# Unscaled rows scattered with three numbers behind each, in a layernorm, scan, attention and expert block

## The chip, the cores and the metric

The kernel runs on one core of one Trainium2 chip. The metric is the device time of one launch in microseconds. PE is TensorE (PEld its weight loads), DVE VectorE, ACT ScalarE, POOL GpSimd and SP SyncE; each takes its instructions in order, and so do the queues on which SP and POOL issue transfers.

## The reference

The input x is (8, 512, 256) in fp32: 8 batches of 512 rows. The result is x + scan(xn) + ffn(xn), where xn is the layernorm of x. What is computed, cut to its core:

```python
# scan branch: A, Bp, Cp, Dp drive a linear recurrence over the 512 rows
u = xn @ W_in + b_in                    # 256 -> 512 channels
u = causal depthwise conv of width 4 (u) + conv_b
h = tanh(A) @ h + u_t * Bp;  y_t = Cp . h + Dp * u_t
scan = silu(y) @ W_out + b_out
# ffn branch: attention plus experts
q, k, v = split(xn @ W_qkv + b_qkv)     # 16 heads of 16
attn = softmax(q k^T / 4) v
gate = softmax(xn @ W_gate + b_gate)    # 8 experts
top_g, top_i = top_k(gate, 2)
moe = sum over the 2 picked experts of top_g * (xn @ W_experts[e] + b_experts[e])
x + scan + attn + moe
```

## The kernel before

**Tiles.** Rows go by 128 on the partitions: NTT = 32 tiles of 128 rows, NT = 4 in each of B = 8 batches. D is 256, E is 8, NJ is 4 (the 256 features as 4 times 64, so that two 64-row matmuls run in two halves of TensorE's rows at a time), S is 512.

**Scan branch.** The recurrence is a lower triangular Toeplitz matrix for each batch (tile ps_zx), followed by the projection with conv (ps_z, L1346; cw is the conv's weights, ys its result on DVE, L1361), a silu by tanh on ACT (th, L1355 and L1371) and the output projection (ps_o, L1384).

**Attention.** There are 32 groups i of 4 heads (4 groups a batch), each in 8 steps s: 256 steps. In a step TensorE forms the scores for the row maximum (maxima, ps_mx, L1533), DVE reduces them (reduce_max, mx, L1545), TensorE forms the transposed scores less that maximum (weights, ps_p, L1571 and L1579), ACT takes the exponential (exponent, p, L1589), and TensorE multiplies by v (values, av, L1598). At the end of a group ACT copies av (av_sb), TensorE transposes it (ps_at), DVE divides by the sums (norm_scale, rsum L1630 and attn L1631) and POOL adds the result to the batch's sum (norm_add, acc, L1641). The q and k of a group come by 16 transfers on SP (load_stack, qs and ks, L1501) from arrays that SP stored before (split, L1480).

**Routing.** With all gates known, DVE picks the two highest of each row (route_pick), counts rows by expert (route_count on TensorE, route_totals), gives each of the 8192 chosen rows a slot in an array sorted by expert (route_slots, key r7) and finds the places to be filled with zeros (route_pads) and the expert of each pair of tiles (wrow, L1139; key r8).

**Experts.** The sorted array xs_d holds NPAIR = 36 pairs of 128-row tiles, each pair of one expert. For each batch, POOL loads the normalised rows (scatter_load, xr, L1163, 512 KB), ACT multiplies each by its gate (scatter_scale, xs, L1170) and POOL scatters them by indirect transfers of 128 rows (place, L1154; 64 for the slots, 16 for the pads). After all of these, each pair is worked on: POOL loads its rows (moe_load, xg, L1189, in 256 B runs) and its expert's weights (wt, L1194, an indirect transfer); TensorE transposes the rows (moe_transpose by turn and tp2, ps_xg, L138 in halves, L150 in whole) with the rows as its stationary operand; ACT copies the result (xgT, L1208); TensorE multiplies (moe_mult, ps_e, L133, a helper's line that other products share); ACT copies (moe_result, y, L1216); SP stores (moe_store, y_d, L1219). In the end POOL gathers the two results of each row and adds them to the batch's sum (combine_gather, L1233). The biases of the experts are added elsewhere, by a small product with the gates (combT).

**Order.** All engines' programs are written in one order by a planner (plan, run_all). Each piece of work is an op: engine, estimated duration, due time "at" in attention steps, the keys that it needs and makes, and the buffers of a ring that it takes and frees. The planner simulates the engines by these estimates, with several settings, and keeps the shortest plan; where TensorE would stand still for long it puts in matmuls on nothing (idle_work, ps_idle, L366). The rings that matter here are attn (2), p (8), xt (2, for xr), big (2, for the scaled rows), stack0 and stack1 (3, the groups' q and k), xg, w, xgT and y (2 each). Changed estimates shift the order of all engines.

Of the kernel before, what the change touches and what calls it, by code (L numbers as in the profile page):

```python
# [12 lines left out]
F32 = mybir.dt.float32  # L13
# [10 lines left out]
def ssm_attention_moe_block(  # L24
# [53 lines left out]
    nc = tc.nc  # L78
# [23 lines left out]
    ppool = ctx.enter_context(tc.tile_pool(name="ppool", bufs=8))  # L102
# [74 lines left out]
    def reach(at):  # L177
# [5 lines left out]
        "m": 3, "mx_m": 1, "p_m": 2, "av": 1, "p": 8, "parts": 2, "mrow": 2, "th": 2, "avsb": 2, "attn": 2,  # L183
# [318 lines left out]
    pad = const.tile([P, 2 * E], I32, name="pad")  # L502
# [516 lines left out]
    def route_pick(i):  # L1019
# [6 lines left out]
        m = tiny("r0", NTT)  # L1026
# [6 lines left out]
        else:  # L1033
            nc.vector.tensor_tensor(rt["z", 2], rt["z", 0], oh, ALU.add)
            nc.vector.tensor_tensor(gates, rt["z", 2], gl, ALU.mult)

# [65 lines left out]
    def route_pads():  # L1102
# [3 lines left out]
        at, lim = tiny("at", 2 * E), tiny("lim", 2 * E)  # L1106
        nc.vector.tensor_tensor(at[:, 0:E], begin_row, count, ALU.add)
        nc.vector.tensor_tensor(
            at[:, E : 2 * E], step[:, 0:E], end[:, E - 1 : E].to_broadcast([P, E]), ALU.add
        )  # L1110
        nc.vector.tensor_scalar(at[:, E : 2 * E], at[:, E : 2 * E], float(P), None, ALU.mult)
        nc.vector.tensor_scalar(at, at, lane, None, ALU.add)
        nc.vector.tensor_scalar(lim[:, 0:E], end, float(P), None, ALU.mult)
        nc.vector.memset(lim[:, E : 2 * E], float(ROWS))
        yield
        ok, spare = tiny("ok", 2 * E), tiny("spare", 2 * E)
        nc.vector.tensor_tensor(ok, at, lim, ALU.is_lt)
        nc.vector.tensor_scalar(spare, step[:, 0 : 2 * E], float(P), float(ROWS), ALU.mult, ALU.add)
        nc.vector.tensor_scalar(spare, spare, lane, None, ALU.add)
# [14 lines left out]
        nc.vector.tensor_reduce(ex, cmp, AX.X, ALU.add)  # L1134

# [8 lines left out]
    NW = 2 * NTT + 2 * E  # L1144
    xs_d = nc.dram_tensor("xs_d", [ROWS + 2 * E * P, D], F32, kind="Internal").ap()
# [15 lines left out]
    def scatter_load(b):  # L1161
        xr[b] = wk2.tile([P, NT, D], F32, tag="x", name=f"xr_{b}")
        nc.gpsimd.dma_start(out=xr[b], in_=rows_of(xn_d[b]))  # L1163

    def scatter_scale(b, i):

        xg_of[b, i] = wk2.tile([P, NT, D], F32, tag="big", name=f"xs_{b}_{i}")
        for t in range(NT):
            n = b * NT + t
            nc.scalar.mul(  # L1170
                xg_of[b, i][:, t, :].rearrange("p (j d) -> p j d", j=NJ),
                xr[b][:, t, :].rearrange("p (d j) -> p j d", j=NJ),
                top[:, i, n : n + 1],
            )
# [695 lines left out]
```

## Time and profile before

| what | value |
|---|---|
| times of three runs | 831.86, 830.24, 823.12 us (median 830.24) |
| profiled execution | 832.42 us, its span 830.7 us, mean granted clock 0.975 |
| busy: PE, DVE, ACT, POOL | 774.7, 534.7, 481.2, 322.6 us |
| the chain that ended last | PE 75%, DVE 9%, ACT 6%, "another core or an unknown queue" 3% |
| scaled copies on ACT (L1170) | 64 of 751 ns, first at 203.2 us, last at 347.5 |
| scatters on POOL (L1154) | 64 of 1036 ns for slots, first at 204.3 us, last at 353.2; 16 for pads |
| loads of sorted rows on POOL (L1189) | 36 of 1318 ns, first at 360.6 us, last at 656.2 |
| gathers of results on POOL (L1233) | 64 of some 1.6 us, nearly all after 680 us |

A span runs from the first to the last instruction of the profiled execution; the time has a little more around it. Busy times are of one engine; "idle before" is the time in which an engine stood before an instruction, put down to what released it. A chain of waits is followed back from the last instruction, and "another core or an unknown queue" is a piece whose releaser the profile can't name. The granted clock is a share of TensorE's full speed.

### The profile page before, as it was taken

How to read it: one execution, taken by the hardware profiler on the slowest of the kernel's cores; microseconds unless marked ns; L12 is line 12 of the kernel's file. 1: busy time of each engine (PE TensorE's matmuls, PEld its weight loads, DVE VectorE, ACT ScalarE, POOL GpSimd, SP SyncE). 2: the span in 40 equal slices, each digit the busy share in tenths (PEclk: the TensorE clock that was granted, in tenths of full speed). 3: DMA queues.
4: the chain of work that ended last, by engine and by line, in shares of the span. 5: the costliest groups of instructions: out<-in, count | busy, mean ns of one | idle time of the engine just before them, and what ended most of it. 6: DMA issues, size and time to landing. Idle time of an engine off the chain costs nothing.

```text
span 830.7 us, 15673 instructions
## 1 busy us (share of the span) xinstructions
PE 774.7 (93%) x6076; PEld 484.3 (58%) x6076; DVE 534.7 (64%) x797; ACT 481.2 (58%) x663; POOL 322.6 (39%) x323
## 2 busy tenths in 40 slices
PE   9998899999897589989999999999999999999997
PEld 8665555555553345446655667665666665555644
DVE  2767776699662474883548654564875557859683
ACT  2536776657775265853656655665575556537363
POOL 4001111011657484543333332332231218388884
PEclk9999999999799598999999999999999999999999
DMA  6757677344656255466967868795855957879754
GB/s 141 200 171 226 165 232 185 98 113 157 188 158 204 82 159 184 130 173 215 239 171 215 221 188 232 191 275 140 251 143 154 258 183 146 234 142 191 150 93 111
DMA packets 115806, 147.67 MB, mean 178 GB/s; under 512 B 33644, under 2 KB 78740, under 8 KB 115733
## 3 DMA queue, kind: packets, MB, share of 16 engines
q1 hardware_dynamic: 93460, 95.28, 40.5%
q0 software_dynamic: 22272, 51.39, 24.8%
q8 instruction: 48, 0.79, 0.4%
q14 instruction: 26, 0.20, 0.1%
HBM read 95.24 MB, written 51.38 MB: 176 GB/s over the span
## 4 chain that ended last, share of the span: by engine, by line
PE 75%; DVE 9%; ACT 6%; another core or an unknown queue 3%; issue 2%; SPq 2%; DMA 1%; POOL 0%; DVEq 0%; ACTq 0%; POOLq 0%
PE av L1598 11%; PE ps_mx L1533 8%; PE ps_p L1571 8%; PE ps_e L133 8%; PE ps_o L1384 7%; PE ps_z L1346 6%; PE ps_p L1579 6%; DVE mx L1545 5%; PE ps_qk L133 5%; PE ps_zx L133 4%; ACT p L1589 3%; PE ps_v L133 3%; PE ps_idle L366 2%; SPq L1501 2%
## 5 line engine op out<-in xcount | busy, mean ns | idle before, releaser
L1545 DVE TENSOR_REDUCE mx<-ps_mx 128x2 f32<-128x1024 f32 x256 | 312.6, 1221 | 180.5 <-PE ps_mx L1533 128.0
L1589 ACT ACTIVATE p<-ps_p 128x1024 f32<-128x1024 f32 x256 | 258.1, 1024 | 95.9 <-PE ps_p L1579 84.0
L1533 PE MATMUL ps_mx<-ks,qs 64*128 64x512 f32 x512 | 124.7, 468 | 22.8 <-DVE mx L1545 18.3
L1571 PE MATMUL ps_p<-qs,ks 64*128 64x512 f32 x512 | 124.2, 472 | 20.9 <-remote 8.7
L1598 PE MATMUL av<-p,v_aug 128*32 128x512 f32 x1024 | 123.3, 599 | 0.0
L1641 POOL TENSOR_TENSOR acc<-acc,attn 128x256 f32<-128x256 f32 x32 | 28.1, 898 | 200.7 <-DVE attn L1631 156.7
L1579 PE MATMUL ps_p<-mrow,pick 64*128 64x512 f32 x512 | 105.2, 397 | 0.0
L1533 PEld LDWEIGHTS ps_mx<-ks,qs 64*128 64x128 f32 x512 | 52.1, 187 | 80.6 <-DVE mx L1545 28.4
L1571 PEld LDWEIGHTS ps_p<-qs,ks 64*128 64x128 f32 x512 | 50.7, 188 | 76.5 <-issue 27.2
L1154 POOL DMA_INDIRECT xs_d<-xs,slot x64 | 66.3, 1036 | 68.0 <-ACT xs L1170 54.2
L1233 POOL DMA_INDIRECT res<-y_d,slot x48 | 76.6, 1595 | 24.2 <-issue 17.6
L1189 POOL DMA_DIRECT2D xg<-xs_d x36 | 47.4, 1318 | 83.3 <-PE ps_xg L138 31.9
L1361 DVE SCALAR_TENSOR_TENSOR ys<-th,cw,ys 128x511 f32<-128x511 f32 (+2 forms) x96 | 72.8, 758 | 1.5
L133 PE MATMUL ps_e<-wt,xgT 64*128 64x256 f32 x576 | 69.6, 380 | 0.0
L1346 PE MATMUL ps_z<-zx,wi 128*128 128x512 f32 x128 | 65.3, 633 | 0.3 <-issue 0.2
L1194 POOL DMA_INDIRECT wt<-in_L_ffn_W_experts_dram,wrow x36 | 35.8, 995 | 68.5 <-PE ps_e L133 29.5
L1384 PE MATMUL ps_o<-wo,ys 128*128 128x256 f32 x256 | 62.1, 387 | 0.0
L133 PEld LDWEIGHTS ps_e<-wt,xgT 64*128 64x128 f32 x576 | 54.3, 186 | 12.6 <-issue 2.3
L1598 PEld LDWEIGHTS av<-p,v_aug 128*32 128x32 f32 x1024 | 26.8, 109 | 54.4 <-issue 53.3
L1579 PEld LDWEIGHTS ps_p<-mrow,pick 64*128 64x128 f32 x512 | 51.4, 189 | 4.6
L1384 PEld LDWEIGHTS ps_o<-wo,ys 128*128 128x128 f32 x256 | 47.4, 194 | 5.4
L133 PE MATMUL ps_qk<-xnTr,wqkv_sb 64*128 64x256 f32 x384 | 47.9, 388 | 2.7 <-ACT xs L1170 1.6
(205 smaller groups left out, 952.1 us busy)
## 6 DMA issues: line engine op xcount, KB each, us to landing
split<-parts SPq DMA_DIRECT2D x32, 512.0 KB
qs<-split SPq DMA_DIRECT2D x248, 64.0 KB
ks<-split SPq DMA_DIRECT2D x248, 64.0 KB
xg<-xs_d POOLq DMA_DIRECT2D x36, 256.0 KB
y_d<-y SPq DMA_DIRECT2D x36, 256.0 KB
xn_d<-xn SPq DMA_DIRECT2D x32, 128.0 KB
acc<-in_L_attn_x_dram SPq DMA_DIRECT2D x8, 512.0 KB
xnr<-xn_d SPq DMA_DIRECT2D x16, 256.0 KB
```

Of the source, the lines that this page charges most:

```text
L133: mm(o, lhsT=lhs, rhs=rhs, start=(j == 0), stop=(j == len(parts) - 1))
L1154: nc.gpsimd.indirect_dma_start(out=xs_views[view], out_offset=bass.IndirectOffsetOnAxis(ap=index, axis=0), in_=src, in_offset=None,)
L1233: nc.gpsimd.indirect_dma_start(out=to[:, t, :], out_offset=None, in_=y_d[:, :], in_offset=bass.IndirectOffsetOnAxis(ap=slot[:, h, n : n + ...
L1346: mm(held["z", b, ct], lhsT=wi[:, c, ct * P : (ct + 1) * P], rhs=zx[b][:, c, :], start=(c == 0), stop=(c == ND - 1),)
L1361: nc.vector.scalar_tensor_tensor(y[:, lag:S], held["th", b, ct][:, 0 : S - lag], cw[:, ct, k : k + 1], bias_tab[:, ct, :] if lag == 0 else ...
L1384: mm(o, lhsT=ys[b][:, ct, t * P : (t + 1) * P], rhs=wo[:, ct, :], start=False, stop=(ct == NCT - 1),)
L1533: mm(ps[:, u, :], lhsT=qs[i % 3][64 * u : 64 * u + 64, pr, t * P : (t + 1) * P], rhs=ks[i % 3][64 * u : 64 * u + 64, pr, :], start=True, s ...
L1545: nc.vector.tensor_reduce(mx[i][:, t, 2 * pr : 2 * pr + 2], held["x", i, s], AX.X, ALU.max, negate=True)
L1571: mm(ps[:, u, :], lhsT=ks[i % 3][64 * u : 64 * u + 64, pr, t * P : (t + 1) * P], rhs=qs[i % 3][64 * u : 64 * u + 64, pr, :], start=True, s ...
L1579: mm(ps[:, u, :], lhsT=pick[64 * u : 64 * u + 64, pr, :], rhs=held["mrow", i, pr][64 * u : 64 * u + 64, :], start=False, stop=True,)
L1589: nc.scalar.activation(p, held["s", i, s], AF.Exp, scale=SCALE)
L1598: mm(av[i][j * HW : (j + 1) * HW, :], lhsT=v_aug[b % 2][:, t, o : o + HW], rhs=pm[i, 2 * t + j // 2][:, j % 2, :], start=(t == 0), stop=(t ...
```

## The change

- Rows are scattered as they are, not scaled. Each row in xs_d is 259 numbers (1036 B) in place of 256: behind the features stand the difference of the two gates, the second gate, and the rank of the first expert. ACT's 64 scaled copies are gone, and the scatters take their rows from xr itself.
- xr is loaded by SP in place of POOL. POOL copies the three numbers behind each row (scatter_tail).
- The pads take 8 transfers in place of 16. route_pads gets a running sum over the experts for it.
- Before the first pair, SP loads all the three-number tails of the sorted rows (tails_load, 9216 runs of 12 B), and DVE makes a gate for each sorted row from them (tails_dve, gate_s): the first gate where the pair's rank is the row's, else the second.
- Sorted rows are loaded by SP in runs of 1 KB (moe_rows); only the weights stay on POOL. The transposes then read every fourth number of a row.
- moe_result is two ACT multiplications by gate_s, 128x256 each, in place of one copy of 128x512.
- The attn ring has 4 buffers in place of 2, the p ring 7 in place of 8. The planner's estimates of the scatters, the loads and the gathers change (0.97 to 1.27, 3.9 to 7.3).

The diff, cut to what matters:

```diff
-    ppool = ctx.enter_context(tc.tile_pool(name="ppool", bufs=8))
+    ppool = ctx.enter_context(tc.tile_pool(name="ppool", bufs=7))
...
-        "m": 3, "mx_m": 1, "p_m": 2, "av": 1, "p": 8, "parts": 2, "mrow": 2, "th": 2, "avsb": 2, "attn": 2,
+        "m": 3, "mx_m": 1, "p_m": 2, "av": 1, "p": 7, "parts": 2, "mrow": 2, "th": 2, "avsb": 2, "attn": 4,
...
@@ -499,7 +499,12 @@
     gates = const.tile([P, NTT, E], F32, name="gates")
     top = const.tile([P, 2, NTT], F32, name="top")
     slot = const.tile([P, 2, NTT], I32, name="slot")
-    pad = const.tile([P, 2 * E], I32, name="pad")
+    pad = const.tile([P, E], I32, name="pad")
+    tails = const.tile([P, NTT, 3], F32, name="tails")
+    ranks = const.tile([P, 2 * NPAIR], F32, name="ranks")
+    gate_s = const.tile([P, 2 * NPAIR], F32, name="gate_s")
     wrow = const.tile([P, NPAIR], I32, name="wrow")
     lane_i = const.tile([P, 1], I32, name="lane_i")
@@ -1023,7 +1028,7 @@
         nc.vector.tensor_tensor(eq, src, wide(top[:, i, :]), ALU.is_equal)
         yield
         nc.vector.tensor_tensor(eq, eq, over(rank), ALU.mult)
-        m = tiny("r0", NTT)
+        m = tails[:, :, 2] if i == 0 else tiny("r0", NTT)
         nc.vector.tensor_reduce(m, eq, AX.X, ALU.max)
         yield
         nc.vector.tensor_tensor(oh, eq, wide(m), ALU.is_equal)
@@ -1033,6 +1038,8 @@
         else:
             nc.vector.tensor_tensor(rt["z", 2], rt["z", 0], oh, ALU.add)
             nc.vector.tensor_tensor(gates, rt["z", 2], gl, ALU.mult)
+            nc.vector.tensor_tensor(tails[:, :, 0], top[:, 0, :], top[:, 1, :], ALU.subtract)
+            nc.vector.tensor_copy(tails[:, :, 1], top[:, 1, :])
     def route_count():
         both = rt["z", 2].rearrange("p t e -> p (t e)")
@@ -1103,20 +1110,27 @@
+        at, lim, none = tiny("at", E), tiny("lim", E), tiny("none", E)
...
+        left, more = tiny("left", E), tiny("more", E)
+        nc.vector.tensor_scalar(left, none, float(P), None, ALU.add)
+        k = 1
+        while k < E:
+            nc.vector.tensor_copy(more[:, 0:k], left[:, 0:k])
+            nc.vector.tensor_tensor(more[:, k:E], left[:, k:E], left[:, 0 : E - k], ALU.add)
+            left, more = more, left
+            k *= 2
...
@@ -1132,6 +1146,7 @@
         yield
         ex = tiny("ex_of", n)
         nc.vector.tensor_reduce(ex, cmp, AX.X, ALU.add)
+        nc.vector.tensor_scalar(ranks, ex, -1.0, float(E), ALU.mult, ALU.add)
         nc.vector.tensor_scalar(ex, ex, float(E - 1), float(P // 2), ALU.min, ALU.mult)
         nc.vector.tensor_scalar(ex, ex, lane64, None, ALU.add)
@@ -1141,8 +1156,10 @@
             )
-    NW = 2 * NTT + 2 * E
-    xs_d = nc.dram_tensor("xs_d", [ROWS + 2 * E * P, D], F32, kind="Internal").ap()
+    NW = 2 * NTT + E
+    XW = D + 3
+    xs_d = nc.dram_tensor("xs_d", [ROWS, XW], F32, kind="Internal").ap()
     xs_views = dram_disjoint_views(xs_d, NW)
     y_d = dram.tile([ROWS, D], F32, name="y_d")
     part_d = dram.tile([B, S, D], F32, name="part_d")
@@ -1159,36 +1176,46 @@
         )
     def scatter_load(b):
-        xr[b] = wk2.tile([P, NT, D], F32, tag="x", name=f"xr_{b}")
-        nc.gpsimd.dma_start(out=xr[b], in_=rows_of(xn_d[b]))
-    def scatter_scale(b, i):
-        xg_of[b, i] = wk2.tile([P, NT, D], F32, tag="big", name=f"xs_{b}_{i}")
-        for t in range(NT):
-            n = b * NT + t
-            nc.scalar.mul(
-                xg_of[b, i][:, t, :].rearrange("p (j d) -> p j d", j=NJ),
-                xr[b][:, t, :].rearrange("p (d j) -> p j d", j=NJ),
-                top[:, i, n : n + 1],
-            )
+        xr[b] = wk2.tile([P, NT, XW], F32, tag="x", name=f"xr_{b}")
+        nc.sync.dma_start(out=xr[b][:, :, 0:D], in_=rows_of(xn_d[b]))
+    def scatter_tail(b):
+        nc.gpsimd.tensor_copy(xr[b][:, :, D:XW], tails[:, b * NT : (b + 1) * NT, :])
     def scatter(b, t, i):
         n = b * NT + t
-        place(2 * n + i, slot[:, i, n : n + 1], xg_of[b, i][:, t, :])
+        place(2 * n + i, slot[:, i, n : n + 1], xr[b][:, t, :])
     def set_zero():
-        rt["zero"] = wk2.tile([P, 2, D], F32, tag="y", name="zero")
+        rt["zero"] = wk2.tile([P, 2, D], F32, tag="y", name="zero").rearrange("p u d -> p (u d)")[:, 0:XW]
         nc.gpsimd.memset(rt["zero"], 0.0)
     def scatter_pads(j):
-        place(2 * NTT + j, pad[:, j : j + 1], rt["zero"][:, 0, :])
+        place(2 * NTT + j, pad[:, j : j + 1], rt["zero"])
+    def tails_load():
+        rt["tails"] = wk2.tile([P, 4 * D], F32, tag="big", name="tails_s")[:, 0 : 3 * 2 * NPAIR]
+        nc.sync.dma_start(
+            out=rt["tails"].rearrange("p (i w) -> p i w", w=3),
+            in_=xs_d.rearrange("(i p) w -> p i w", p=P)[:, :, D:XW],
+        )
+    def tails_dve():
+        v = rt["tails"].rearrange("p (i w) -> p i w", w=3)
+        nc.vector.tensor_tensor(gate_s, v[:, :, 2], ranks, ALU.is_equal)
+        nc.vector.tensor_tensor(gate_s, gate_s, v[:, :, 0], ALU.mult)
+        nc.vector.tensor_tensor(gate_s, gate_s, v[:, :, 1], ALU.add)
+    def moe_rows(k):
+        xg[k] = wk2.tile([P, 2 * D], F32, tag="xg", name=f"xg_{k}")
+        nc.sync.dma_start(
+            out=xg[k].rearrange("p (u d) -> p u d", u=2),
+            in_=xs_d[2 * k * P : 2 * (k + 1) * P, 0:D].rearrange("(u p) d -> p u d", u=2),
+        )
     def moe_load(k):
-        xg[k] = wk2.tile([P, NJ, 2, P // 2], F32, tag="xg", name=f"xg_{k}")
-        nc.gpsimd.dma_start(
-            out=xg[k], in_=xs_d[2 * k * P : 2 * (k + 1) * P, :].rearrange("(u p) (j d) -> p j u d", u=2, j=NJ)
-        )
         wt[k] = wk2.tile([P, NJ, D], F32, tag="w", name=f"wt_{k}")
         nc.gpsimd.indirect_dma_start(
@@ -1200,7 +1227,7 @@
     def moe_transpose(k):
         held["xg", k] = turn(
-            f"ps_xg_{k}", [lambda r, j=j: xg[k][r, j].rearrange("p u d -> p (u d)") for j in range(NJ)]
+            f"ps_xg_{k}", [lambda r, j=j: xg[k][r].rearrange("p (m j) -> p j m", j=NJ)[:, j, :] for j in range(NJ)]
         )
     def moe_evict(k):
@@ -1213,7 +1240,9 @@
     def moe_result(k):
         res["y", k] = wk2.tile([P, 2, D], F32, tag="y", name=f"y_{k}")
-        nc.scalar.copy(res["y", k], held["e", k][:, :, 0:D])
+        for u in range(2):
+            n = 2 * k + u
+            nc.scalar.mul(res["y", k][:, u, :], held["e", k][:, u, 0:D], gate_s[:, n : n + 1])
     def moe_store(k):
         nc.sync.dma_start(
@@ -1266,27 +1295,31 @@
     def scatter_ops(b, at):
         X = ("xt", "xr", b)
-        op("pool", 0.83, at, lambda: scatter_load(b), needs=[("xn_d", b), "r7"], makes=[("xr", b)], takes=[X], kb=512)
+        op("sp", 0.5, at - 2, lambda: scatter_load(b), needs=[("xn_d", b), "r2"], makes=[("xr", b)], takes=[X], kb=512)
+        op("pool", 0.25, at, lambda: scatter_tail(b), needs=[("xr", b), "r4"], makes=[("xt", b)])
         for i in range(2):
-            G = ("big", "xs", b, i)
-            op("act", 1.5, at, lambda i=i: scatter_scale(b, i), needs=[("xr", b)], makes=[("xs", b, i)], takes=[G], frees=[X])
             for t in range(NT):
-                op("pool", 0.97, at, lambda t=t, i=i: scatter(b, t, i), needs=[("xs", b, i)], makes=["placed"], frees=[G], kb=128)
+                op("pool", 1.27, at, lambda t=t, i=i: scatter(b, t, i), needs=[("xt", b), "r7"], makes=["placed"], frees=[X], kb=128)
         if b == B - 1:
             Z = ("y", "zero")
             op("pool", 0.52, at, set_zero, makes=["zero"], takes=[Z])
-            for j in range(2 * E):
-                op("pool", 0.97, at, lambda j=j: scatter_pads(j), needs=["zero", "r8"], makes=["placed"], frees=[Z], kb=128)
+            for j in range(E):
+                op("pool", 1.27, at, lambda j=j: scatter_pads(j), needs=["zero", "r8"], makes=["placed"], frees=[Z], kb=128)
     placed = "all_placed"
     def moe_ops(k, at):
         G, W, T, Y = ("xg", k), ("w", k), ("xgT", k), ("y", k)
-        op("pool", 1.8, at - 3, lambda: moe_load(k), needs=[placed] + reach(at - 8), makes=[("moe", k)], takes=[G, W], kb=768)
-        op("pe", 0.5, at, lambda: moe_transpose(k), needs=[("moe", k)], makes=[("moet", k)], takes=[("mt", "xg", k), T], frees=[G])
+        if k == 0:
+            Z = ("big", "tails")
+            op("sp", 0.4, at - 4, tails_load, needs=[placed], makes=["tails"], takes=[Z], kb=700)
+            op("dve", 0.5, at - 3, tails_dve, needs=["tails", "r8"], makes=["gate_s"], frees=[Z])
+        op("sp", 0.4, at - 3, lambda: moe_rows(k), needs=[placed] + reach(at - 8), makes=[("moex", k)], takes=[G], kb=256)
+        op("pool", 1.27, at - 3, lambda: moe_load(k), needs=["r8"] + reach(at - 8), makes=[("moew", k)], takes=[W], kb=512)
+        op("pe", 0.5, at, lambda: moe_transpose(k), needs=[("moex", k)], makes=[("moet", k)], takes=[("mt", "xg", k), T], frees=[G])
         op("act", 0.59, at, lambda: moe_evict(k), needs=[("moet", k)], makes=[("moeT", k)], frees=[("mt", "xg", k)])
-        op("pe", 1.75, at, lambda: moe_mult(k), needs=[("moeT", k)], makes=[("moep", k)], takes=[("m", "e", k), Y], frees=[W, T])
-        op("act", 0.59, at, lambda: moe_result(k), needs=[("moep", k)], makes=[("moey", k)], frees=[("m", "e", k)])
+        op("pe", 1.75, at, lambda: moe_mult(k), needs=[("moeT", k), ("moew", k)], makes=[("moep", k)], takes=[("m", "e", k), Y], frees=[W, T])
+        op("act", 0.85, at, lambda: moe_result(k), needs=[("moep", k), "gate_s"], makes=[("moey", k)], frees=[("m", "e", k)])
         op("sp", 0.4, at + 0.5, lambda: moe_store(k), needs=[("moey", k)], makes=[("y_d", k)], frees=[Y], kb=256)
     def combine_ops(b, at):
@@ -1298,7 +1331,7 @@
         into = ("acc", b) if late else ("res", b)
         for h in range(2):
             op(
-                "pool", 3.9, at - 3 + h, lambda h=h: combine_gather(b, h),
+                "pool", 7.3, at - 3 + h, lambda h=h: combine_gather(b, h),
                 needs=ys_all + reach(at - 6 + h) + [("moe_in", b, h - 1) if h else into], makes=[("moe_in", b, h)], kb=512,
             )
         if not late:
-        o = held["attn", i] = wk2.tile([P, 4 * NT * HD], F32, tag="attn", name=f"attn_{i}", bufs=2)
+        o = held["attn", i] = wk2.tile([P, 4 * NT * HD], F32, tag="attn", name=f"attn_{i}", bufs=4)
```

## The prediction

> **What bounds the kernel now.** I read the page's totals and its 40 slices first.
>
> ```profile
> span 830.7 us, 15673 instructions
> PE 774.7 (93%) x6076; PEld 484.3 (58%) x6076; DVE 534.7 (64%) x797; ACT 481.2 (58%) x663; POOL 322.6 (39%) x323
> PE   9998899999897589989999999999999999999997
> POOL 4001111011657484543333332332231218388884
> PEclk9999999999799598999999999999999999999999
> ```
>
> TensorE is the bound almost everywhere; only slices 11 to 14 (some 205 to 310 us) fall to 7, 5 and 8, and there POOL rises and the granted clock drops. So I asked for the busy time by window.
>
> ```profile
> core 0: us, PE busy (x) PEld busy (x) DVE busy (x) ACT busy (x) POOL busy (x), PEclk, DMA share, GB/s
> 120.00:200.00 80.00, 77.28 (x622) 44.12 (x618) 61.25 (x132) 50.38 (x73) 7.58 (x16) 1.00 0.51 147
> 200.00:260.00 60.00, 55.17 (x364) 33.92 (x364) 39.32 (x54) 44.09 (x62) 36.07 (x36) 0.91 0.54 171
> 260.00:320.00 60.00, 40.61 (x223) 22.50 (x216) 30.18 (x42) 30.52 (x43) 36.57 (x38) 0.77 0.42 132
> 320.00:365.00 45.00, 41.53 (x265) 21.21 (x263) 33.37 (x42) 32.02 (x45) 24.79 (x25) 0.96 0.49 157
> 500.00:680.00 180.00, 177.17 (x1469) 116.43 (x1466) 108.41 (x131) 105.44 (x141) 45.00 (x42) 1.00 0.75 208
> ```
>
> Columns: stretch, length, busy time of each engine, granted clock. From 500 on TensorE is 98% busy with the experts mixed in. From 200 to 365, while rows are scattered, it isn't. Taking off the fill matmuls of L366 (5.37, 0.60 and 0 us there, 2.54 before 200) and multiplying by the clock, an estimate of work at full clock: 49.80 x 0.91 + 40.01 x 0.77 + 41.53 x 0.96 = 45.3 + 30.8 + 39.9 = 116.0 us in 165, or 70%. The 80 us before have (77.28 - 2.54)/80 = 93%. The loss is some 40 us, and I looked for its causes in the groups (line, what it writes from what, shapes, count | busy us, mean ns | idle before) and in the chain of waits, by time (start, us, what).
>
> ```profile
> L1170 ACT ACTIVATE xs<-xr,top 128x256 f32<-128x256 f32 x64 | 42.9, 751 | 0.0
> L823 ACT ACTIVATE xn<-x,rs 128x256 f32<-128x256 f32 x32 | 16.9, 590 | 7.0 <-POOL rs L815 6.8
> L1154 POOL DMA_INDIRECT xs_d<-xs,slot x64 | 66.3, 1036 | 68.0 <-ACT xs L1170 54.2
> L1189 POOL DMA_DIRECT2D xg<-xs_d x36 | 47.4, 1318 | 83.3 <-PE ps_xg L138 31.9
> L138 PEld LDWEIGHTS ps_xg<-ident,xg 64*128 64x128 f32 x232 | 11.2, 138 | 6.2 <-ACT p L1589 1.6 <-issue 1.5 <-PE ps_mx L1533 0.5
> ```
>
> ```profile
> 261.54 10.15 another core or an unknown queue
> 271.71 0.26 DVE rsum L1630
> ...
> 275.51 7.66 another core or an unknown queue
> 283.20 1.24 DVE mx L1545
> ```
>
> Two causes show. POOL's scatters stand 54.2 us waiting for ACT's scaled copies, and ACT's in-order queue holds those copies (four per group, 2.6 us on the chain at 218 and 236 us) between the exponentials that TensorE needs. And there are the pieces without a releaser, 18.7 us of chain between 195 and 290: VectorE waits for matmuls long started, and goes on (271.71, 283.20) near the end of a run of back-to-back scatters and pads on POOL (250.9 to 281.4 us).
>
> **The change, part by part.**
>
> *Scaling taken off ACT.* 64 copies, 42.9 us of ACT in 150 us, are gone, with the waits of scatter on copy and of copy on the "big" buffers. Scatters then follow POOL's own pace, 0.96 + 0.30 us: 72 x 1.27 = 91 us in place of 204 to 354. For the stretch I take the rate of 320 to 365, where scatters still run but no piece without a releaser shows: 39.9/45 = 88.6%. 116.0/0.886 = 130.9 us against 165: -34.1. The bounds are 0 (nothing of the loss was due to it) and the 93% of before 200: 116.0/0.934 = 124.2, -40.8. The attn ring of 4 belongs here: POOL's adds L1641 stand between scatters, and DVE's next group no longer waits for them; in the same sum. The p ring of 7 instead of 8 costs nothing while av follows exp within 7 steps; without that, TensorE would stand one exp, 1.02 us, a time.
>
> *Routing.* Some 12 more small DVE operations (prefix sum, ranks, tails) at 0.2 us, as L1139 and L1136 take: +2.4. They lie on the chain (195 to 203 us is DVE), so I count all of it. Slots are needed for the scatter, wrow no more.
>
> *xr to SyncE, tails on POOL.* POOL loses 8 x 0.83 us and gets 8 copies of 128x12, by its row L1641 (128x256, 0.73 to 0.90) under 0.9 each. On SP each xr load waits until the eight scatters of two batches earlier have landed; behind it in the queue stand the stack loads of L1501 (16 issues of 0.42 us a group), and ps_mx and ps_p wait for those. A batch of scatters takes 10 us; the loads run up to three groups ahead and one group of eight steps takes about 20 us, so I put it at 0. Without that lead it costs up to 10 us once or twice.
>
> *Tails.* One transfer of 9216 runs of 12 B, behind all scatters and ahead of the first rows on SP. 576 runs on each of 16 DMA engines at 9 ns (the 16 B packets of this trace) to 18.8 ns (the conv weight's load, 512 runs of 16 B): 5.2 to 10.8 us. Only the first results y wait for it, but ACT's queue, exps too, waits behind y. Between 0 and 10.8 I take +3, since transposes and products of two pairs go first.
>
> *Sorted rows on SyncE.* POOL loses 47.4 us; SP gains 36 issues of 0.4 us; packets of 1 KB (53 ns) take 16 x 53 = 0.85 us of an engine in place of 64 x 19 = 1.2. Rows stand behind stores of y (L1219, waits 54.1 us for y) and ahead of stack loads. With TensorE 98% busy and two buffers this gives nothing; if a row load slips behind a store, one pair (2 to 3 us) is late, and attention steps fill in.
>
> *Strided transposes.* Eight 64-wide loads a pair now read every fourth number. No PE read of that kind is in this trace. The nearest row is ACT's: 128x256 read with that stride 751 ns, contiguous (L823) 590, x1.27. On the transposes' matmuls and loads (12.1 + 4.6 and 11.2 + 2.9 = 30.8 us, a good half of it hidden by overlap) that is about +5. Bounds: 0, and 14.1 x 3 = +42 if a load takes four times as long, as the four-times-wider span read would make it. Below nothing is excluded: the same numbers are read. TensorE being 98% busy there, it is all exposed.
>
> [...]
>
> *Results.* Two ACT operations of 128x256 in place of one 128x512 copy (586 ns): by the slope from 512 to 1024 columns (1024 - 586) a 256-wide one is 0.37, by L823 0.59; +0.15 to +0.6 us x 36 = 5 to 21 us of ACT. ACT is 59% busy in 500 to 680 and TensorE hides it: 0; without that cover, up to that much.
>
> *Pads, scatter width.* Eight transfers fewer are in the 72 above. A 1036 B row costs 8 packets an engine at 112 ns = 0.9 us a transfer, under POOL's pace of 1.27.
>
> Sum: 832.4 (the profiled execution's own time) - 34.1 + 2.4 + 3 + 5 = 808.7. It lay 2.2 above the median of 830.24, so the forecast is 806.5; bounds without a rival: 832.4 - 40.8 - 2.2 = 789, and 843 with transposes at +42.
>
> **The rivals.**
>
> (a) The pieces without a releaser stay as large as they were: 806.5 + 18.7 = 825. For it: they go with scatters and pads, which remain. Against: the half of the pads.
>
> (b) They grow; this is the slower side. Scatters now stand back to back for 91 us. In the run of 250.9 to 281.4 us, 17.8 of 30.5 us (58%) were lost. The same share of 91 is 53: 808.7 + 53 - 2.2 = 860. It decides from 26% on ((832.4 - 808.7)/91). Against: the runs of 204 to 216 us and of 344 to 354 (eight scatters) show no such piece, and none stands in the gathers at the end, where POOL is 80% busy.
>
> (c) The strided loads cost the upper bound: 843. It decides from +29 on, about 0.8 us a pair.
>
> (d) The change doesn't free the stretch, because SP's queue is late instead: 10 to 20 us of the 34 come back as waits of ps_mx for stack loads: 817 to 827.
>
> **How the numbers follow.** Forecast 0.60, (a) 0.11, (b) 0.14, (c) 0.08, (d) 0.07. The three times shown lie 1% apart, so 1% is what can be told from no change (822 to 838.5). Faster: the forecast and a part of (d), 0.63. Same: (a), the rest of (d), 0.13. Slower: (b), (c) and little else, 0.24. The range runs from 788 over (a), (d) and (c) to 843; (b) is left out. The forecast's own range is 789 to 820.
>
> **What would show it.** Right: no xs on ACT; POOL's scatters over within some 110 us of the first; TensorE's work at full clock in that stretch near 88%; first expert matmul some 40 us earlier; ps_xg weight loads near 175 ns (138 before). Wrong: pieces without a releaser over 25 us in all (b); ps_xg loads over 300 ns (c); idle time of ps_mx ended by DMA (d); y waiting over 10 us for gate_s.

## The result, and the profile after

| | changed | before | ratio, 95% interval |
|---|---|---|---|
| recorded runs | 856.5 us (851.4 to 867.1) | 829.1 us (823.1 to 831.9) | 1.032 (1.023 to 1.041) |
| repeated on another chip | 802.6 us (801.9 to 803.1) | 806.7 us (803.1 to 811.2) | 0.994 (0.992 to 0.996) |

The same two kernels stand in the other order on another chip. Over all runs the kernel before takes about 806 us on some chips (medians of 806.1 and 806.7 on two) and about 829 on others (829.1 in the recorded runs, and 829.0 to 830.2 on three chips, one of which came twice and was the same both times, 830.2 and 829.9). I call them quiet and loud chips; whether it is the chip itself or what else went on in it, no run tells. Every ratio below is against the kernel before as it ran beside it on the same chip. The recorded profile after is the longest of its runs (867.1 us), which the ratio leaves out, so its sizes are cross-checked with a second loud profile below.

The page after, recorded (loud):

```profile
span 865.4 us, 15414 instructions
PE 796.4 (92%) x5994; PEld 492.6 (57%) x5994; DVE 535.2 (62%) x809; ACT 451.2 (52%) x635; POOL 258.0 (30%) x279
PE   9998999997779797699999999999999999999797
POOL 4001111005471707111111111110110115477885
PEclk9999998998879879699999999999999999999899
PE 73%; DVE 7%; another core or an unknown queue 5%; ACT 3%; POOL 3%; issue 3%; SPq 3%; DMA 2%; DVEq 0%; ACTq 0%; POOLq 0%
```

The hole in TensorE's row is not filled; it is wider (the 10th to the 17th slice, some 195 to 368 us). ACT has 30 us less to do, and POOL's scatters stand in three bursts, but nothing was gained by it. Windows of the same profile, columns as in the prediction:

```profile
200.00:260.00 60.00, 43.46 (x223) 21.84 (x220) 29.14 (x56) 17.59 (x22) 36.08 (x41) 0.80 0.48 156
260.00:320.00 60.00, 51.65 (x277) 27.71 (x278) 34.35 (x46) 22.86 (x30) 19.67 (x21) 0.86 0.45 147
320.00:365.00 45.00, 31.50 (x172) 18.39 (x172) 20.43 (x27) 12.37 (x15) 19.56 (x22) 0.81 0.35 110
500.00:680.00 180.00, 178.23 (x1412) 119.03 (x1408) 110.29 (x135) 106.64 (x155) 22.92 (x25) 1.00 0.65 193
```

The stretch with the experts (500 to 680) is as full as before. The chain of waits between 195 and 365 us (start, us, what) says what the hole is:

```profile
by line: another core or an unknown queue 27.0%; PE ps_z L1379 12.9%; PE ps_o L1417 7.9%; PE ps_mx L1566 7.2%; PE av L1631 6.6%; PE ps_p L1604 6.5%; PE ps_qk L133 6.1%; ACT p L1622 4.9%; PE ps_p L1612 4.5%; DVE mx L1578 2.9%; issue 2.5%; PE
200.28 6.45 another core or an unknown queue
214.27 4.21 another core or an unknown queue
...
248.06 13.10 another core or an unknown queue
287.01 9.61 another core or an unknown queue
...
341.88 10.06 another core or an unknown queue
```

27% of 170 us, 46 us, are pieces without a releaser, of 4.2 to 13.1 us among those above: DVE or ACT waits for a matmul that was started long ago and sees it late. Before there were 22 us of them. The timeline around the longest shows it (start, us, what):

```profile
247.43 0.47 PE L1566 MATMUL ps_mx<-ks,qs 64*128 64x512 f32 x2
261.18 1.23 DVE L1578 TENSOR_REDUCE mx<-ps_mx 128x2 f32<-128x1024 f32 x1 [12.40 <-remote]
```

The product is done at 247.90 us, and DVE, idle for 12.4 us, starts on it 13.3 us later. On a quiet chip the same pair stands 0.09 us apart (217.08 and 217.17 us in r_after).

### The profile page after: what moved, and what is told of

The parts are those of the page before. It is cut to its first block, busy times and chain, and to the rows that moved or that the text cites. A ratio compares the mean times of both kernels' runs of the same rounds, so it can differ in the third digit from the quotient of the medians.

```text
span 865.4 us, 15414 instructions
## 1 busy us (share of the span) xinstructions
PE 796.4 (92%) x5994; PEld 492.6 (57%) x5994; DVE 535.2 (62%) x809; ACT 451.2 (52%) x635; POOL 258.0 (30%) x279
## 4 chain that ended last, share of the span: by engine, by line
PE 73%; DVE 7%; another core or an unknown queue 5%; ACT 3%; POOL 3%; issue 3%; SPq 3%; DMA 2%; DVEq 0%; ACTq 0%; POOLq 0%
PE av L1631 11%; PE ps_p L1604 8%; PE ps_mx L1566 7%; PE ps_z L1379 7%; PE ps_e L133 7%; PE ps_qk L133 6%; PE ps_o L1417 6%; PE ps_p L1612 5%; DVE mx L1578 4%; PE ps_zx L133 3%; PE ps_v L133 3%; ACT p L1622 2%; PE ps_idle L366 2%; POOL acc L1262 2%
## 5 line engine op out<-in xcount | busy, mean ns | idle before, releaser
L1604 PE MATMUL ps_p<-qs,ks 64*128 64x512 f32 x512 | 127.5, 482 | 17.0 <-ACT p L1622 10.6
L1566 PE MATMUL ps_mx<-ks,qs 64*128 64x512 f32 x512 | 126.7, 475 | 13.6 <-DVE mx L1578 6.7
L1631 PE MATMUL av<-p,v_aug 128*32 128x512 f32 x1024 | 131.6, 611 | 1.7 <-issue 1.3
L1612 PE MATMUL ps_p<-mrow,pick 64*128 64x512 f32 x512 | 107.4, 402 | 1.6 <-issue 1.6
L1379 PE MATMUL ps_z<-zx,wi 128*128 128x512 f32 x128 | 70.5, 677 | 18.9 <-DVE acc L1427 16.1
L1171 POOL DMA_INDIRECT xs_d<-xr,slot x64 | 62.8, 982 | 56.8 <-DMA xr<-xn_d 28.7
L1379 PEld LDWEIGHTS ps_z<-zx,wi 128*128 128x128 f32 x128 | 23.6, 205 | 46.1 <-issue 25.0
```

Source lines behind the costliest of these rows:

```text
L1171: nc.gpsimd.indirect_dma_start(out=xs_views[view], out_offset=bass.IndirectOffsetOnAxis(ap=index, axis=0), in_=src, in_offset=None,)
L1379: mm(held["z", b, ct], lhsT=wi[:, c, ct * P : (ct + 1) * P], rhs=zx[b][:, c, :], start=(c == 0), stop=(c == ND - 1),)
L1566: mm(ps[:, u, :], lhsT=qs[i % 3][64 * u : 64 * u + 64, pr, t * P : (t + 1) * P], rhs=ks[i % 3][64 * u : 64 * u + 64, pr, :], start=True, s ...
L1604: mm(ps[:, u, :], lhsT=ks[i % 3][64 * u : 64 * u + 64, pr, t * P : (t + 1) * P], rhs=qs[i % 3][64 * u : 64 * u + 64, pr, :], start=True, s ...
L1612: mm(ps[:, u, :], lhsT=pick[64 * u : 64 * u + 64, pr, :], rhs=held["mrow", i, pr][64 * u : 64 * u + 64, :], start=False, stop=True,)
L1631: mm(av[i][j * HW : (j + 1) * HW, :], lhsT=v_aug[b % 2][:, t, o : o + HW], rhs=pm[i, 2 * t + j // 2][:, j % 2, :], start=(t == 0), stop=(t ...
```

## Where the time went, by attention steps

The start of the exponential of some attention steps, in us, in profiles of both kernels on both kinds of chip:

| step | before, quiet | changed, quiet | before, recorded | changed, recorded |
|---|---|---|---|---|
| 56 | 194.3 | 195.0 | 192.5 | 197.5 |
| 72 | 244.1 | 237.6 | 247.1 | 269.6 |
| 96 | 326.3 | 315.6 | 351.4 | 380.1 |
| 136 | 458.6 | 441.2 | 484.7 | 505.7 |
| 248 | 781.1 | 776.6 | 807.1 | 841.5 |

Between steps 56 and 96 the kernel before takes 132.0 us on the quiet chip and 158.9 in the recorded profile; the changed one 120.6 and 182.6. The rest runs alike on both: up to step 56 they are within 2.5 us of each other, and from step 104 to 248 the kernel before stays 26 us behind its quiet self, the changed one 64 to 65. The scatter stretch makes the difference.

## The experiments

### The kernels once more: r_after, r_before

> The changed kernel as it is, beside the kernel before once more: in the last runs the kernel before took 806 us and not 829, and no kernel of that call had pieces without a releaser. Theory A2 (those pieces belong to the state in which the first profiles were taken, and denser scatters get more of them): where the kernel before takes 806 us, the changed one takes 800 to 806 and has no such pieces; where the kernel before takes 829, it takes 851 or more. Rival (the changed kernel is slower by itself): 825 us or more beside 806.

Measured: 802.6 us, 0.994 (0.992 to 0.996), no piece without a releaser.

> The kernel before as it is, for its profile beside the others of this call. Theory A2: near 806 us, no pieces without a releaser between 195 and 365 us, TensorE's share in that stretch at 85% or more in place of 70%, since the 54 us of waits for ACT's copies remain. Rival (the pieces are part of the kernel): they stand at 256 to 283 us as in the first profile.

Measured: 806.2 us, no such piece either. Windows of the quiet profiles, the kernel before first:

```profile
200.00:260.00 60.00, 55.11 (x381) 33.56 (x381) 44.28 (x62) 47.77 (x67) 38.30 (x38) 0.97 0.60 187
260.00:320.00 60.00, 56.22 (x362) 31.74 (x361) 44.33 (x58) 44.82 (x65) 48.12 (x48) 0.97 0.62 200
320.00:365.00 45.00, 42.03 (x307) 25.68 (x305) 29.03 (x37) 25.95 (x36) 19.08 (x18) 0.96 0.64 187
```

```profile
200.00:260.00 60.00, 57.18 (x395) 33.20 (x394) 48.46 (x78) 31.43 (x40) 43.27 (x47) 1.00 0.78 231
260.00:320.00 60.00, 59.62 (x394) 33.17 (x392) 51.27 (x66) 32.33 (x42) 37.11 (x37) 1.00 0.75 190
320.00:365.00 45.00, 45.00 (x367) 32.22 (x366) 24.03 (x35) 25.66 (x41) 8.49 (x9) 1.00 0.78 226
```

With the prediction's formula (fill taken off, 6.5 and 2.4 us, times clock) the work at full clock is 142 of 165 us before and 159 after: here the change does fill the stretch, 86% to 97%. The first profile's 70% was the chip's doing for the larger part, and so were the waits for ACT's copies: POOL's scatters wait 28.7 us for them here in place of 54.2. POOL's scatters before stand as dense here as there (250 to 281 us has its like at 249 to 281), so density alone isn't enough: it needs the loud chip.

### One part alone, quiet chips

**e3_before_unscaled**: the kernel before without ACT's copies, and the planner told 1.27 us for a scatter in place of 0.97.

```diff
...
-        place(2 * n + i, slot[:, i, n : n + 1], xg_of[b, i][:, t, :])
+        place(2 * n + i, slot[:, i, n : n + 1], xr[b][:, t, :])
...
```

> The kernel before with one edit: ACT's scaled copies are left out and the scatters take the unscaled rows from xr, so gates are not applied. Rows of 1024 B, 16 pads, loads of xr and of sorted rows on POOL and contiguous transposes as before. Theory A: the scatters stand denser than before, pieces without a releaser grow from 19 to 40 us or more, and the time is 835 us or more although 43 us of ACT work are gone. If the density is harmless and the loss comes from the other edits (SP's queue, tails, strided transposes), 800 to 815 us.

Measured: 798.2 us, 0.989 (0.985 to 0.993). On the quiet chip the copies on ACT's queue, with the order that goes with them, are worth 8 us of path. The 800 to 815 us expected for harmless density were written for a kernel of 829 us; the growth of the pieces could not show here.

**e1_rows_1k**: rows of 1024 B.

```diff
-    xs_d = nc.dram_tensor("xs_d", [ROWS, XW], F32, kind="Internal").ap()
+    xs_d = nc.dram_tensor("xs_d", [ROWS, D], F32, kind="Internal").ap()
...
-        place(2 * n + i, slot[:, i, n : n + 1], xr[b][:, t, :])
+        place(2 * n + i, slot[:, i, n : n + 1], xr[b][:, t, 0:D])
...
```

> The changed kernel with rows of 1024 B in place of 1036: the three numbers behind each row are not scattered, so the gates that the results are multiplied by are not the right ones. Theory A (back-to-back index transfers of POOL delay the moment at which the other engines see TensorE's results, whatever the row is): 850 to 860 us, and the chain between 195 and 365 us keeps 40 to 60 us of pieces without a releaser. Theory B (rows that don't start on a round address are what is slow): those pieces fall to the 19 us of before or less and the time to 825 us or less.

Measured: 802.8 us, 0.995 (0.993 to 0.997), as the changed kernel's 0.994. The 12 bytes cost nothing here. On this quiet chip it could not tell theory A from B, since there was nothing to explain.

**e6_contiguous**: the price of the strided reads.

```diff
-            f"ps_xg_{k}", [lambda r, j=j: xg[k][r].rearrange("p (m j) -> p j m", j=NJ)[:, j, :] for j in range(NJ)]
+            f"ps_xg_{k}", [lambda r, j=j: xg[k][r, j * P : (j + 1) * P] for j in range(NJ)]
```

> The changed kernel, but the transposes of sorted rows read 128 neighbouring numbers in place of every fourth, which gives the products the wrong features; all else is the same. If strided weight loads lie on the path (213 ns each in the changed kernel, 138 contiguous in the one before): 75 ns x 8 to 10 loads x 36 pairs, at most 20 us, of which about half shows: 8 to 12 us less than the changed kernel. If they hide behind the matmuls: within 2 us of it.

Measured: 799.5 us beside 802.6. The groups of the changed kernel's quiet profile, then of this one (busy us, mean ns):

```profile
L138 PE MATMUL ps_xg<-ident,xg 64*128 64x64 f32 x136 | 10.4, 272 | 0.0
L138 PEld LDWEIGHTS ps_xg<-ident,xg 64*128 64x128 f32 x136 | 10.4, 206 | 2.2 <-issue 1.3
```

```profile
L138 PE MATMUL ps_xg<-ident,xg 64*128 64x64 f32 x136 | 7.2, 225 | 0.0
L138 PEld LDWEIGHTS ps_xg<-ident,xg 64*128 64x128 f32 x136 | 6.5, 138 | 2.8 <-issue 1.3
```

The stride makes a load 206 ns in place of 138, the 128-wide form 209 in place of 140. The 212 loads are some 14.5 us longer in sum, and 3.1 us of it shows: most of a load lies beside matmuls.

**e5_runs_256**: contiguous by smaller runs and weights copied into another order.

```diff
...
+            in_=w_exp[e].rearrange("(j p) f -> p j f", j=NJ),
...
+        op("sp", 0.5, 36 + e, lambda e=e: permute(e), makes=["w_rows"], kb=512)
```

> The changed kernel with contiguous transposes in another way: SyncE loads the sorted rows in runs of 256 B (two transfers a pair) as the kernel before did on POOL, and the experts' weights are copied once into the order that this needs (eight transfers of 256 KB early on). If the strided loads cost 8 to 12 us and smaller runs cost nothing: 8 to 10 us less than the changed kernel. If smaller runs or the doubled issue on SyncE cost what the stride saves: no difference.

Measured: 816.4 us, 1.011 (1.007 to 1.014). Step 16 already comes at 98.3 us in place of 84.9, long before any expert, so the order or the copies cost it and nothing is learned of the transposes.

### Loud chips: what draws the pieces

The changed kernel itself ran on a loud chip in the recorded runs alone. The variants of this section that are said to have run on a loud chip ran on three chips, which count as loud because the kernel before took 829.0 to 830.2 us (medians) beside them.

**e9_attn_2**: the changed kernel, attn ring 2 (the words that change; the tile's buffers likewise).

```diff
-"attn": 4
+"attn": 2
```

> The changed kernel with an attn ring of 2 in place of 4 (p ring 7). If POOL's adds behind scatters hold up VectorE: waits of attn for POOL appear in the scatter stretch and it takes 806 us or more. If a ring of 2 is enough once scatters don't wait for ACT: within 2 us of the changed kernel's 802.6.

Measured: 855.1 us, 1.028 (1.024 to 1.033), beside the changed kernel's 1.032 on a loud chip: the ring is no visible part of it. Its profile is the second loud one: 40 us of pieces, and 54 us behind the quiet changed kernel from step 88 on, where the recorded profile (10 us longer) has 64.

**e10_before_attn_4**: the kernel before with attn 4 and p 7.

> The kernel before with the changed rings alone (attn 4, p 7). If the ring is a part of the gain: 2 to 4 us less than the kernel before. If ACT's copies hold all that can be gained in the scatter stretch: no difference, within 1.5 us.

Measured: 821.3 us, 0.990 (0.986 to 0.994). It has 11 us of pieces in place of 22, which is more than the 8 us gained, so the gain may come from other moments of the scatters and not from the ring. Open.

**e7_runs_256_spread** (the edit is against e5_runs_256) and **e8_more_traffic**:

```diff
-        op("sp", 0.5, 36 + e, lambda e=e: permute(e), makes=["w_rows"], kb=512)
+        op("sp", 0.5, 34 + 5 * e, lambda e=e: permute(e), makes=["w_rows"], kb=512)
```

> As the version with runs of 256 B and copied weights, but the eight copies of weights are spread over attention steps 34 to 69, where DMA is half idle, in place of steps 36 to 43. That version lost 15 us between steps 8 and 16, long before the first expert, so it told nothing of the transposes. If the copies' place was its fault and contiguous transposes are worth their 3 us: 799 to 801 us where the changed kernel takes 802.6. If the order of the plan is what was lost: 810 us or more.

Measured: 867.1 us, 1.046 (1.039 to 1.053), with the pieces of a loud chip (up to 10.2 us each). Step 16 comes at 83.8 us again, so it was the place of the copies, with the plan that goes with it, that cost e5_runs_256 its start; for the transposes the run tells nothing.

```diff
...
+    for n in range(32):
+        op("sp", 0.4, 58 + 1.4 * n, lambda n=n: more(n), makes=[("more", n)], kb=512)
```

> The changed kernel with 32 extra copies of 256 KB from DRAM to DRAM on SyncE's queue during attention steps 58 to 101, the stretch of the scatters. If a loaded memory path is what makes the pieces without a releaser (and makes update records of the semaphores go missing, as 880 of 930 of TensorE's were left in the first profile of the changed kernel): pieces of 5 us and more appear, update records are missing, 820 us or more. If traffic of the same core can't make them: no such pieces, all records there, and only waits for transfers grow, 803 to 815 us.

Measured: 904.6 us, 1.090 (1.083 to 1.098). Step 56 is 38 us late before any large piece, so most of the loss is not the pieces; of these there are 42 us, up to 15.7 us each. Whether traffic makes pieces can't be told from a chip that has them anyway.

**d1_plain_pool** (e4_plain_pool on a quiet chip before): the same rows by plain transfers.

```diff
-        nc.gpsimd.indirect_dma_start(
-            out=xs_views[view],
-            out_offset=bass.IndirectOffsetOnAxis(ap=index, axis=0),
-            in_=src,
-            in_offset=None,
-        )
+        nc.gpsimd.dma_start(out=xs_d[view * P : (view + 1) * P, :], in_=src)
```

> The changed kernel with plain transfers by POOL's queue in place of the index transfers: the same sources, sizes and order, but each 128 rows go to the next 128 rows of xs_d, so the rows are not sorted by expert. Theory A in the narrow form (it is the index transfers): the pieces without a releaser vanish between 195 and 365 us, and the time is 800 to 820 us, or near 835 if strided transposes and SP's queue cost 30. In the wide form (any row write of POOL's queue delays): the pieces stay, 850 us or more.

Measured on a quiet chip: 802.3 us, 0.994 (0.992 to 0.996).

> The version with plain transfers by POOL's queue (rows unsorted) once more, meant for a chip on which the kernel before takes 829 us. There, if index transfers draw the pieces without a releaser: none between 195 and 365 us, all update records there, about 802 us as on the other chips. If any row write of that queue draws them: 845 us or more, as the changed kernel.

Measured on a loud chip: 802.3 us, 0.975 (0.964 to 0.986). Its chain by engine has no unknown piece at all:

```profile
PE 77%; DVE 9%; POOL 3%; ACT 3%; issue 3%; DMA 2%; SPq 2%; DVEq 0%; POOLq 0%; ACTq 0%
```

The order, the sources and the bytes are those of the changed kernel (2304 packets of 4144 B in both traces), and the plain transfers stand closer (seven in 3.84 us). Against the changed kernel's 856.5 us on another loud chip 54 us are gone. Writes of that size and density drew no piece here; the index transfers drew 46 us of them in the recorded profile and 40 in that of e9_attn_2, on other loud chips. With the index went the scattered places of the rows in DRAM, and which of the two matters was not tried.

**d2_spaced** (e2_spaced on a quiet chip before): after each scatter four fills on POOL of a tile that nothing reads (planner told 2.6).

```diff
         place(2 * n + i, slot[:, i, n : n + 1], xr[b][:, t, :])
+        for _ in range(4):
+            nc.gpsimd.memset(spacer, 0.0)
...
```

> The changed kernel with four small fills of 128x256 on POOL after each scatter, so that scatters start about 2.5 us apart and not 1.27. Theory A: with room between the transfers the pieces without a releaser go (under 10 us in all), though the scatters now take 180 us, and the time is below 845 us. If the number of transfers or their bytes are what delays and not their density, the pieces stay at 40 us or more and the time at 855 us or more.

Measured on a quiet chip: 827.1 us, 1.023 (1.019 to 1.028).

> The version with four fills after each scatter, meant for a chip on which the kernel before takes 829 us. There, if the density of scatters draws the pieces: under 10 us of them, 827 to 835 us as on the other chips (827). If each scatter draws its share whatever the distance: 850 to 890 us.

Measured on a loud chip: 828.1 us, 1.000 (0.996 to 1.005), no piece. With 2.57 us between starts the loud chip is as fast as the quiet one. The price on a quiet chip is 25 us; the scatters end late (389 us), and the plan is another one.

**f1_two_fills, f2_one_fill**, both on a loud chip: two fills (planner told 1.9), one fill (told 1.6).

> The changed kernel with two fills of 128x256 (0.31 us each) on POOL after each scatter: starts some 1.9 us apart, the scatters over in about 140 us. Where the kernel before takes 806 us: 803 to 810, as the plan is little longer than the changed kernel's. Where it takes 829: if 1.9 us is room enough, no pieces without a releaser and 803 to 810 us; if the room has to be 2.5 us, 10 to 40 us of pieces and 815 to 845.

Measured: 814.3 us, 0.984 (0.977 to 0.992), no piece.

> The same with one fill: starts some 1.6 us apart. Where the kernel before takes 806 us: 801 to 808. Where it takes 829: if the delay fades gradually with distance, about half of the changed kernel's pieces, 20 to 30 us, and 820 to 835; if it has a sharp edge below 1.6 us, none and 801 to 808; if the edge lies above, 850 or more.

Measured: 812.7 us, 0.983 (0.975 to 0.991), no piece. POOL's timeline (start, us, what), first of the recorded profile after, then of this kernel:

```profile
249.21 0.96 POOL L1171 DMA_INDIRECT xs_d<-xr,slot  x1 [0.31 <-issue]
250.47 0.96 POOL L1171 DMA_INDIRECT xs_d<-xr,slot  x1 [0.30 <-issue]
```

```profile
285.21 0.97 POOL L1172 DMA_INDIRECT xs_d<-xr,slot  x1 [0.17 <-issue]
286.17 0.34 POOL L1190 MEMSET spacer<- 128x256 f32 x1
286.67 0.97 POOL L1172 DMA_INDIRECT xs_d<-xr,slot  x1 [0.17 <-issue]
```

Starts 1.27 us apart drew 46 us of pieces in the first, 1.46 us apart none in the second.

**g1_one_fill_same_order, g2_one_fill_146**, on a loud chip: one fill, planner told 1.27 and 1.46.

> The changed kernel with one fill of 128x256 after each scatter and the planner's estimate left at 1.27, so that the order of all engines is the changed kernel's and only the distance grows to 1.46 us (measured in the version with one fill). No pieces without a releaser on any chip. If the order was what cost 10 us: 803 to 807 us. If the later end of the scatters (72 x 0.19 = 14 us) is what costs: 811 to 816.

Measured: 813.0 us, 0.981 (0.974 to 0.988), no piece. All engines have the changed kernel's order here, so neither the absence of pieces nor the price of the pause comes from another order. It follows the quiet changed kernel 13.0 us behind from step 104 to 232, near the 72 x 0.19 = 14 us of the second expectation. 8.1 us of it are lost by step 96; between 96 and 104 the chain waits 7.7 us for the first sorted rows (at 336.31 us), which the quiet changed kernel's doesn't.

> The same with the planner told 1.46 in place of 1.6. No pieces on any chip. If a truer estimate gives a better order: 803 to 809 us; if the order of a plan is luck of some 10 us: anywhere between 802 and 816.

Measured: 817.2 us, 0.985 (0.977 to 0.993), no piece. A truer estimate gives no better order.

No piece does not mean no delay. In g1_one_fill_same_order smaller delays are left, which the profile puts down to the product itself, as here:

```profile
308.51 0.40 PE L1571 MATMUL ps_mx<-ks,qs 64*128 64x512 f32 x2
309.99 1.22 DVE L1583 TENSOR_REDUCE mx<-ps_mx 128x2 f32<-128x1024 f32 x1 [1.28 <-PE ps_mx L1571]
```

The product is done at 308.91 us and DVE starts 1.08 us later. Counted over the traces from 190 to 430 us (each of TensorE's updates from the end of the latest matmul before it that makes one, so at least this late):

| profile, loud chips | starts apart, us | updates over 0.5 us late | largest delay, us |
|---|---|---|---|
| changed, recorded | 1.27 | 36 | 9.6 |
| e9_attn_2 | 1.27 | 27 | 12.6 |
| e8_more_traffic | 1.27 | 18 | 16.0 |
| e7_runs_256_spread | 1.27 | 32 | 12.2 |
| before, recorded | 1.27 in bursts | 17 | 7.7 |
| e10_before_attn_4 | 1.27 in bursts | 22 | 8.9 |
| f2_one_fill | 1.46 | 17 | 1.5 |
| g1_one_fill_same_order | 1.46 | 14 | 1.8 |
| g2_one_fill_146 | 1.46 | 13 | 1.7 |
| f1_two_fills | 1.83 | 0 | none |
| d2_spaced | 2.57 | 1 | 0.7 |
| d1_plain_pool | 0.53, no index | 0 | none |

The profiles of the quiet chips have none. So the delay shrinks with distance, and between 1.27 and 1.46 us most of it goes (7.7 to 16.0 us at the largest, then 1.5 to 1.8), but not all.

On a loud chip the changed kernel with one fill of 0.33 us after each scatter is 17 us faster than the kernel before: the change's 3.2% loss becomes a gain of 1.9%. It was not run on a quiet chip. The versions with plain transfers (802.3 us on both) and with four fills (827.1 and 828.1) take the same on both kinds. By that it would take 813 us there, slower than both kernels, less what the small delays cost it on the loud chip; this is an estimate. No version that computes the result was shown to beat both kernels on both kinds of chip.

## Why the prediction was wrong, by its own steps

- **The term of -34.1 is the step that failed**, in "For the stretch I take the rate of 320 to 365, where scatters still run but no piece without a releaser shows". It let the pieces go together with ACT's copies, and gave no reason for it. They are two things. In the recorded profiles steps 56 to 96 grew by 23.7 us (158.9 to 182.6) where the term had them shrink. On the quiet chip, which has no pieces, they shrink by 11.4 us (132.0 to 120.6), a third of the term, and at the end the change is 4 us faster (806.7 to 802.6). The loud chips lengthen these steps by 27 us in the kernel before (158.9 against 132.0) and by 54 (e9_attn_2) to 62 us (recorded) in the changed one. Most of the "some 40 us" of loss that the profile showed was never ACT's.
- **Rival (b) came out.** It priced the pieces at 58% of 91 us, 53 us, and the total at 860; measured were 40 to 46 us of pieces, 54 to 62 us of longer stretch, and 856.5. That the total fits so well is partly luck: its base of 806.5 is 4 us above the quiet changed kernel, and the recorded stretch lost more than 53. Its mechanism, index transfers back to back, is shown by d1_plain_pool and g1_one_fill_same_order, but only for loud chips; that a chip could be without the pieces was in no rival. What spoke against it in the text, that some runs of eight scatters had no piece, was true and not enough; it got 0.14 where the evidence for it, pieces that end with the scatters, stood in the fence. The 18.7 us that rival (a) adds is a misreading: 18.7 is the share in percent of the 95 us looked at, and the two pieces are 10.15 + 7.66 = 17.8 us.
- **The scatters' own pace** was right: on the quiet chip 72 in 108 us (first start 195.5, last 303.8), for "within some 110 us"; on the loud one 150, with waits of 28.7 us for loads of xr and of 24.4 us in POOL's adds for attn. The first transpose for the experts comes 22 us earlier on the quiet chip (343.6 to 321.4) and 16 us later in the recorded profiles (369.6 to 385.9), where 40 earlier were forecast.
- **Strided transposes**: +5 forecast, 3.1 measured, on the path three fifths of what ACT's row gave, though a load grew by half (138 to 206 ns) and not by 1.27. The upper bound of +42 was far off: that a load grows with the span it reads was the author's estimate, and no run shows it (206 ns in place of 138 for a span four times as wide).
- **Tails**: +3 forecast, none seen. gate_s is made 13 us after the issue (307.3 to 320.3 us, quiet), beyond the upper bound of 10.8, but the first y starts at 325.3 and waits for ps_e alone.
- **Routing**: +2.4 forecast; step 56 is 0.7 us later on the quiet chip. Not separated from the order.
- **Results**: 2 x 471 - 586 = 356 ns a pair, 13 us of ACT in all, within the 5 to 21 and hidden as said. ACT's waits for y are waits for ps_e.
- **SP's queue**, rival (d): no wait of ps_mx for a stack load appears among TensorE's waits; one wait of scatters for xr on the quiet chip is 5.1 us.
- **After the stretch** the quiet lead of 17.4 us at step 136 shrinks to 4.5 at step 248. About 1 us of that is the stride (e6_contiguous is 1.7 us ahead at step 136 and 2.6 at 248); the rest was not taken apart.

## What to carry to other kernels

Time that a profile can't give to an instruction must not be put into the term of the edit beside it: it needs a price and a chance of its own, for going, staying and growing. Before a stretch that is odd (a low clock, pieces without a releaser) is taken for the kernel's, run the same kernel on a second chip. And where an engine's queue issues a long run of index transfers, try a short pause after each, on both kinds of chip: here one fill decides the sign on a loud chip (1.032 without it, 0.981 with it), and four fills cost 25 us on a quiet one.

## What the runs showed of the hardware

- On the loud chips index scatters of 128 rows that start 1.27 us apart make other engines see TensorE's results up to 13 us late (16 in e8_more_traffic). At 1.46 us 1.8 us at most are left, at 1.83 us nothing over 0.5 us, and beside plain transfers 0.53 us apart nothing over 0.5 us either. On the quiet chips none of it shows at 1.27 or at 2.57 us. How a scatter on POOL's queue holds up TensorE's updates stays open. In the recorded profile after, some updates stand 1.43 us apart (217.04, 218.47, 219.90 us); from 195 to 420 us a distance of 1.40 to 1.46 us occurs 6 times there and never in r_after. That a service of 1.43 us per transfer falls behind at 1.27 would fit; it is an argument and was not tried.
- The index gathers at the kernel's end, 1.6 us each and some 1.9 us from start to start, drew no piece and no late update in any profile.
- Traces of the loud chips lack records: 91% to 95% of the updates of TensorE's instructions are there (842 of 926 for d2_spaced, 880 of 930 for the changed kernel, 884 of 930 for d1_plain_pool); on a quiet chip the changed kernel has 930 of 930. d1_plain_pool lacks them with no piece, so they mark the chip and not the delay.
